# A decoder layer on one core: instructions on separate regions of one tile are declared independent

## The chip, the core and the metric

The kernel runs on one core of one Trainium2 chip. The metric is the time on the device in microseconds (us) of one execution. Five engines work side by side, each through its own list of instructions in order: TensorE (PE in the profile; PEld is its loading of weights), VectorE (DVE), ScalarE (ACT), GpSimd (POOL) and SyncE (SP), which here only issues transfers (DMA). They hold each other back by waits on semaphores, which stand in the program at the instruction that waits.

## The reference

One transformer decoder layer with a mixture of experts, on 32 sequences of 128 tokens with 128 features, in float32, 16 heads of 8:

```python
x = _layernorm(x + _attn(x, x, x, sa_*, causal=True), ln1_g, ln1_b)
x = _layernorm(x + _attn(x, encoder_output, encoder_output, ca_*, causal=False), ln2_g, ln2_b)
x = _layernorm(x + _moe(x, router_w, router_b, e_w1, e_b1, e_w2, e_b2), ln3_g, ln3_b)
```

`_attn` projects queries, keys and values, takes `softmax(q k / sqrt(8))` by head, and projects the result with `wo`. `_moe` routes every token to the best 2 of 8 experts; an expert is 128 to 512, gelu, 512 to 128, with biases; the two results are added with a softmax of the two router weights.

## The kernel before

**Stages.** The 32 sequences form 8 groups of 4 (`gi`). A group goes through self attention (`"s"`) and, two turns later, cross attention (`"c"`); the turns are s0 s1 s2 c0 s3 c1 ... s7 c5 c6 c7, and steps of both kinds are interleaved. Up to about 436 us into the span this attention part runs. Then come 71 blocks of 128 routed rows, each with one expert's weights: transpose the rows (line 1778), move them out of PSUM (1781), first product (1793), gelu (1801), second product (1810), bias (1822), scatter of the results (1827). The blocks overlap, and the layer norms of finished groups lie between them.

**Scores.** Each attention step computes the scores twice. Once by query, from which DVE takes the negated maximum of each row (line 995); the maxima are split into two bfloat16 numbers by POOL (1013, 1019), transposed by PE (1027) and copied by ACT (`nmT`, 1034 to 1038). Then by key, with the maxima added by further matmuls, so that ACT can take the exponentials straight from PSUM (1436) and PE can use them as they lie. All these matmuls are issued by the helper `mm`, so they share line 891; their operands tell them apart.

**One tile with several regions.** The tile `wall` (128 x 8 x 1156 numbers) holds the eight experts' weights at the end. Before that its middle holds three regions of 2048 numbers, `km_t[0]` to `km_t[2]`:

```python
km0 = [KM0 + 4 * G * P * i for i in range(3)]
km_t = [wflat[:, o : o + 4 * G * P].rearrange("p (r n) -> p r n", r=4) for o in km0]
```

Regions 0 and 1 take the masked keys of self attention, of even and odd groups: `masks` (line 724) writes them with four DMAs from `k` (in the profile `wall<-k`; the same helper writes the masked queries, `qm<-q`). Region 2 takes the keys of cross attention split into three bfloat16 parts: `parts` computes them, writes them to `k_d` in memory (861) and `spread` (868) reads them back with four DMAs (`wall<-k_d`). The self steps (`emit_step`, operand `wall,q`) read regions 0 and 1, the cross steps (`emit_cross`, operands `qm` and `wall`) read region 2. What a step reads and what the helpers write for another group thus lie apart, in one tile.

**PSUM.** There are four pairs of banks, `sc0` to `sc3`. A step of scores takes a whole pair (`pairs`); everything else takes half a pair, one bank (`singles`), and at most two pairs are broken up so. Two tasks that have nothing to do with each other may hold the two halves of one tile.

**The order.** Every piece of work is a `Task` with an engine, an estimated duration, a priority, the tasks it depends on (`deps`) and the places it uses (`bufs`). `Plan.run` makes the order of all tasks by a list schedule; in it the two halves of a pair, and the regions of `wall`, are separate places. `Plan.emit` then issues the tasks in this order. The waits are not made by the plan but from the tiles that the issued instructions name: in the program before, an instruction on a part of a tile also waits where an instruction queued earlier touched another part of it, as the rows of the next section but one show.

Of the kernel before, what the change touches and what calls it, by code (L numbers as in the profile page):

```python
# [136 lines left out]


class Task:
    __slots__ = ("eng", "dur", "fn", "deps", "bufs", "prio", "lat", "mode", "use", "ni", "n", "next", "end", "start")  # L140

    def __init__(self, eng, dur, fn, deps, bufs, prio, lat, mode, use, ni):
        self.use, self.ni = use, ni
        self.eng, self.dur, self.fn, self.bufs = eng, dur, fn, bufs
        self.prio, self.lat, self.mode = prio, lat, mode
        self.deps = [d for d in deps if d is not None]
        self.next, self.end, self.start = [], None, None


class Plan:  # L150
# [3 lines left out]
    def __init__(self):  # L154
        self.tasks = []

    def add(self, eng, dur, prio, fn, deps=(), bufs=(), lat=0.0, mode=None, use=0.0, ni=0):
        t = Task(eng, dur, fn, deps, list(bufs), prio, lat, mode, use, ni)
        for b in t.bufs:
            b.left += 1  # L160
        self.tasks.append(t)
        return t
# [100 lines left out]
        self.order = order  # L263
        return max(t.end for _, _, t in order)

    def emit(self):
        for _, _, t in self.order:
            t.fn()


@with_exitstack
def kernel(
# [34 lines left out]
    nc = tc.nc  # L307
# [13 lines left out]
    plan = Plan()  # L321
    add = plan.add
# [89 lines left out]
    t_selc = early("DVE", 0.6, 4.2, c_selc, [t_cols])  # L412
# [123 lines left out]
    bqk = sb([P, 8], "bqk")  # L536
    bqc = sb([P, 1], "bqc")

    def pe(dur, prio, fn, deps, bufs, mode="128x128", use=None, ni=0):
        use = max(dur - 0.18, 0) if use is None else use  # L540
        return add("PE", dur, prio, fn, deps, bufs, mode=mode, use=use, ni=ni or int(dur * 18))

    b = Buf(singles)

# [172 lines left out]
    def masks(dst, src, bufs, prio, deps, two):  # L717

        ts = []
        for q, rs in (("SP", (0, 2)), ("ACT", (1, 3))) if two else (("SP", range(4)),):  # L720

            def fn(q=q, rs=rs):
                for r in rs:
                    (nc.sync if q == "SP" else nc.scalar).dma_start(out=dst.at[r::4, r, :], in_=src()[r::4])

            ts.append(add(q, 0.6 * len(rs), prio, fn, deps, bufs, lat=2.0))
        return ts

    def prepare(kind, gi, n_=1):
# [111 lines left out]
    def parts(w, gi, bank, dep, bcol, t_bias, to, prio):  # L841
# [25 lines left out]
                src = d[:, a[0] : a[0] + 2] if a[1] > a[0] else bc(d[:, a[0]], 1, 2)  # L867
                nc.sync.dma_start(out=view(to)[c::4], in_=src)  # L868

        return [add("SP", 4 * 0.6, prio + 0.06, spread, [tw], [to], lat=5.5)]  # L870

    def sq_cols(tl):

# [109 lines left out]
    def step_use(sq, sk):  # L983
        return (0.43 if sq is not None else 0) + (0.55 if sk is not None else 0)
# [461 lines left out]
    def self_step(sq, sk, i):  # L1446
# [5 lines left out]
        for h in range(2):  # L1452
# [7 lines left out]
            if sk is not None:  # L1460
# [6 lines left out]
            t = pe(  # L1467
                step_time(sq, sk), i + 0.5 * h + PR["score"],
                lambda sq=sq, h=h, qp=qp, sk=sk, kp=kp: emit_step(sq, h, qp, sk, kp), deps, bufs, "32x64",
                use=step_use(sq, sk), ni=step_instr(sq, sk),  # L1470
            )
            if sq is not None:
                last_sq.setdefault(sq[1] % 2, []).append(t)
# [8 lines left out]
    def cross_step(tl, i):  # L1482
# [5 lines left out]
        for h in range(2):  # L1488
            qp = Buf(pairs)
            t = pe(  # L1490
                0.38, i + 0.5 * h + PR["cscore"], lambda h=h, qp=qp: emit_cross(False, h, gi, w, qp),
                [*it.t_q, *it.t_km], [qp, it.qm, it.km], "64x128", use=0.21, ni=16,
            )
            last_sq.setdefault(2, []).append(t)
            ms.append(maximum(tl, h, qp, nm, i + 0.5 * h + PR["cmax"], t))
        transposed_maxima(tl, i, nm, ms)
        i += NL
        for h in range(2):
            kp = Buf(pairs)
            t = pe(  # L1500
                0.6, i + 0.5 * h + PR["ckey"], lambda h=h, kp=kp: emit_cross(True, h, gi, w, kp),
                [*it.nmt[tl], t_selc], [kp, it.qm, it.km, it.nmT, it.pr[w]], "64x128", use=0.42, ni=32,
            )
            last_sq.setdefault(2, []).append(t)
            exponentials(tl, h, kp, t, i + 0.5 * h + PR["cexp"])
# [398 lines left out]
        final(gi, s, 2 if gi == NG - 1 else 1)  # L1904

    plan.run()
    plan.emit()


# [39 lines left out]
```

## Time and profile before

| | |
|---|---|
| median of 3 runs | 665.37 us (664.6, 665.37, 671.98) |
| the profiled execution | 662.87 us, its span 661.2 us |
| mean granted TensorE clock in it | 0.905 |
| PE busy | 513.9 us, 78% of the span |
| DVE, ACT, POOL busy | 425.8, 332.6, 318.5 us |
| attention part | about 0 to 436 us |
| blocks of the experts | about 436 to 640 us |
| tail | 640 to 661 us |

The span is measured from the first instruction to the last; 1.67 us of the execution lie around it. In answers by window the columns are the busy time of each engine with its count of instructions, then the mean granted clock of TensorE (1.00 is full speed), the mean busy share of the DMA engines and the gigabytes per second they moved. In answers on waits a row reads: engine and line, whom it waited for, the total in us, how often, the longest. In a timeline the brackets at the end give the idle time just before and what ended it.

### The profile page before, as it was taken

How to read it: one execution, taken by the hardware profiler on the slowest of the kernel's cores; microseconds unless marked ns; L12 is line 12 of the kernel's file. 1: busy time of each engine (PE TensorE's matmuls, PEld its weight loads, DVE VectorE, ACT ScalarE, POOL GpSimd, SP SyncE). 2: the span in 40 equal slices, each digit the busy share in tenths (PEclk: the TensorE clock that was granted, in tenths of full speed). 3: DMA queues.
4: the chain of work that ended last, by engine and by line, in shares of the span. 5: the costliest groups of instructions: out<-in, count | busy, mean ns of one | idle time of the engine just before them, and what ended most of it. 6: DMA issues, size and time to landing. Idle time of an engine off the chain costs nothing.

```text
span 661.2 us, 20553 instructions
## 1 busy us (share of the span) xinstructions
PE 513.9 (78%) x8055; PEld 397.7 (60%) x8055; DVE 425.8 (64%) x1091; ACT 332.6 (50%) x742; POOL 318.5 (48%) x473
## 2 busy tenths in 40 slices
PE   8997898768777867877798885848579898978830
PEld 5655666546555645654667654637568887877730
DVE  7534769467477668457548876755446557866885
ACT  3352656446256443436545462526146666666642
POOL 8210431422236455225315536746757455767583
PEclk9997999879799977879988987779879999999985
DMA  4552141413213412341532416141222122333331
GB/s 111 155 167 82 55 125 43 129 41 105 83 34 110 118 45 58 106 117 26 134 106 62 129 50 178 48 126 53 77 61 58 57 63 81 105 102 95 107 92 57
DMA packets 55209, 58.67 MB, mean 89 GB/s; under 512 B 7951, under 2 KB 47927, under 8 KB 53064
## 3 DMA queue, kind: packets, MB, share of 16 engines
q1 hardware_dynamic: 50308, 48.49, 25.9%
q0 software_dynamic: 4320, 8.47, 3.8%
q8 instruction: 63, 1.03, 0.7%
q10 hardware_dynamic: 484, 0.39, 0.2%
q14 instruction: 34, 0.28, 0.1%
HBM read 35.69 MB, written 17.90 MB: 81 GB/s over the span
## 4 chain that ended last, share of the span: by engine, by line
PE 44%; DVE 17%; ACT 14%; issue 8%; DMA 7%; POOL 3%; SPq 2%; another core or an unknown queue 2%; DVEq 1%; ACTq 0%; POOLq 0%
PE sc L891 22%; PE sc L1810 5%; ACT pr L1436 5%; PE sc L1793 5%; ACT k L1801 4%; DVE nm L995 4%; DMA wall<-k_d 3%; PE sc L709 2%; PE sc L702 2%; PE sc L788 2%; PE sc L712 2%; SPq L868 2%; DVE y L1867 1%; DVE y L1864 1%
## 5 line engine op out<-in xcount | busy, mean ns | idle before, releaser
L995 DVE TENSOR_REDUCE nm<-sc 128x8 f32<-128x1024 f32 (+1 forms) x112 | 133.3, 1215 | 77.0 <-PE sc L891 71.7
L1436 ACT ACTIVATE pr<-sc 128x1024 f32<-128x1024 f32 x112 | 112.0, 1023 | 103.0 <-PE sc L891 85.3
L1827 POOL DMA_INDIRECT res_d<-o,id x71 | 84.7, 1192 | 53.2 <-DVE o L1822 29.3
L1801 ACT ACTIVATE k<-sc,qm 128x128 f32<-128x128 f32 x284 | 78.5, 379 | 57.0 <-PE sc L1793 35.8
L1810 PE MATMUL sc<-qm,k 128*128 128x128 f32 x568 | 80.0, 285 | 16.7 <-ACT k L1801 9.7
L1810 PEld LDWEIGHTS sc<-qm,k 128*128 128x128 f32 x568 | 70.8, 195 | 25.9 <-ACT k L1801 17.0
L1345 POOL DMA_INDIRECT rows_d<-x,rid x64 | 65.9, 1029 | 35.6 <-issue 21.4
L1793 PE MATMUL sc<-q,qm 128*128 128x128 f32 x568 | 74.5, 284 | 3.6 <-DVE qm L1772 2.3
L1793 PEld LDWEIGHTS sc<-q,qm 128*128 128x128 f32 x568 | 70.4, 200 | 4.5 <-DVE qm L1772 2.6
L891 PE MATMUL sc<-pr,v 128*32 128x128 f32 (+1 forms) x2048 | 66.4, 274 | 6.2 <-issue 2.0
L891 PE MATMUL sc<-wall,q 32*64 32x512 f32 (+1 forms) x512 | 56.1, 530 | 15.8 <-DMA wall<-k_d 15.7
L891 PEld LDWEIGHTS sc<-pr,v 128*32 128x32 f32 x2048 | 52.3, 115 | 17.2 <-issue 7.3
L891 PE MATMUL sc<-qm,k 32*64 32x256 f32 (+1 forms) x512 | 54.1, 515 | 8.1 <-DVE nm L995 4.0
L1772 DVE COPY qm<-wall 128x1156 f32 x71 | 55.3, 779 | 3.5 <-DVE y L1231 1.0
L1822 DVE TENSOR_TENSOR o<-sc,qm 128x128 f32<-128x128 f32 x71 | 20.4, 288 | 50.7 <-PE sc L1810 23.7
L891 PE MATMUL sc<-wall,qm 64*128 64x128 bf16 x512 | 26.8, 238 | 21.4 <-DMA wall<-k 7.0
L1781 ACT ACTIVATE q<-sc,col_b,col_g 128x128 f32<-128x128 f32 x71 | 33.1, 475 | 19.1 <-PE sc L1778 13.5
L1019 POOL CAST nmx<-nm 128x16 bf16<-128x16 f32 x32 | 6.4, 201 | 69.5 <-DVE nm L995 67.8
L1166 ACT ACTIVATE y<-y,rs 128x128 f32<-128x128 f32 x64 | 27.6, 490 | 24.4 <-DVE rs L1158 24.3
L891 PEld LDWEIGHTS <-qm 64*128 64x128 bf16 x512 | 18.6, 103 | 33.9 <-issue 31.8
L1098 DVE STREAM_TRANSPOSE u<-sc 128x512 f32<-128x512 f32 x32 | 22.8, 711 | 21.3 <-PE sc L891 8.9
L891 PE MATMUL sc<-qm,wall 64*128 64x128 bf16 x512 | 28.0, 232 | 6.8 <-ACT pr L1436 3.7
(260 smaller groups left out, 987.2 us busy)
## 6 DMA issues: line engine op xcount, KB each, us to landing
wall<-k_d SPq DMA_DIRECT2D x32, 256.0 KB
qm<-q_d SPq DMA_DIRECT2D x32, 256.0 KB
wall<-in_L_xattn_e_w_dram SPq DMA_DIRECT2D x16, 256.0 KB
pr<-res_d SPq DMA_DIRECT2D x7, 512.0 KB
k_d<-sp SPq DMA_DIRECT2D x8, 384.0 KB
q_d<-sp SPq DMA_DIRECT2D x8, 384.0 KB
xin<-rows_d SPq DMA_DIRECT2D x36, 65.0 KB
xT<-rows_d SPq DMA_DIRECT2D x35, 65.0 KB
```

What stands on the lines that cost most here:

```text
L891: nc.tensor.matmul(out_, lhsT=lhsT, rhs=rhs, start=start, stop=stop, skip_group_check=True)
L995: lambda: nc.vector.tensor_reduce(dst(), src(), AX.X, ALU.max, negate=True), [dep], [pair, nm],
L1098: t = add("DVE", dve(512), prio, lambda: nc.vector.transpose(u1.at, bank.at), [dep], [bank, u1])
L1166: lambda i=i: nc.scalar.activation(to()[:, i, :], y.at[:, i, :], AF.Identity, bias=rs.at[:, 1, i : i + 1], scale=rs.at[:, 0, i : i + 1],),
L1345: ins = nc.gpsimd.indirect_dma_start(out=rows_d[:, :], out_offset=bass.IndirectOffsetOnAxis(ap=rid.at[:, i, k : k + 1], axis=0), in_=x2g[g ...
L1436: lambda: nc.scalar.activation(prb.at[:, 8 * h : 8 * h + 8, :].rearrange("p h q -> p (h q)"), pair.at.rearrange("p b n -> p (b n)"), AF.Ex ...
L1772: nc.vector.tensor_copy(w.at.rearrange("p r n -> p (r n)")[:, 0:WB], flat[:, bass.ds(r, WB)])
L1781: lambda: nc.scalar.activation(xT.at[:, 0:P], bt.at[:, 0:P], AF.Identity, bias=cols["b2"], scale=cols["g2"]),
L1793: nc.tensor.matmul(pp.at[:, 0, c * P : (c + 1) * P], lhsT=wv()[:, c * P : (c + 1) * P], rhs=xT.at[:, 0:P], start=True, stop=True)
L1801: nc.scalar.activation(h.at[:, c, :], pp.at[:, 0, c * P : (c + 1) * P], AF.Gelu, bias=wv()[:, 2 * FF + c : 2 * FF + c + 1],)
L1810: nc.tensor.matmul(pp.at[:, 1, 0:P], lhsT=h.at[:, c, :], rhs=wv()[:, FF + c * P : FF + (c + 1) * P], start=c == 0, stop=c == NFC - 1,)
L1827: ins = nc.gpsimd.indirect_dma_start(out=res_d[:, :], out_offset=bass.IndirectOffsetOnAxis(ap=idb.at[:, 0:1], axis=0), in_=o.at, in_offset ...
```

## The change

A task may carry `apart=(join, off)`: it joins the named group, and it is declared independent of the instructions that joined group `off` before. Four names are used: `masked` (the DMAs of `masks`) against `csteps` (cross steps), and `spread` (the DMAs of `spread`) against `steps` (self steps), in both directions. For the halves of PSUM pairs `emit` makes the groups itself: a task that holds half `j` of a pair is declared independent of what another engine did on half `1 - j`. In both cases dependencies are kept on tasks that stand in `deps` or share a place. The plan, the priorities and the computation stay as they are.

```diff
     def emit(self, nc, tc):
+        of = {}
         for _, _, t in self.order:
+            t.made = made = []
+            nc.push_inst_callback(made.append)
             t.fn()
+            nc.pop_inst_callback()
+            join, off = [t.apart[0]], [t.apart[1]]
+            for b in t.bufs:
+                if isinstance(b.slots, Banks.Kind) and b.slots.single:
+                    entry, j, _ = b.slots.b.of[id(b.at)]
+                    join.append((id(entry[0]), j, t.eng))
+                    off += [(id(entry[0]), 1 - j, e) for e in ("PE", "ACT", "DVE") if e != t.eng]
+            join = {g for g in join if g}
+            off = {g for g in off if g and g in of} - {(*g[:2], e) for g in join if len(g) == 3 for e in ("PE", "ACT", "DVE")}
+            places = {id(b.at) for b in t.bufs}
+            for g in off:
+                keep = [
+                    i for u in of[g] if u in t.deps or any(id(b.at) in places for b in u.bufs) for i in u.made
+                ]
+                for i in made:
+                    tc.declare_no_dep(i, group=str(g), keep=keep, reason="apart within a tile")
+            for g in join:
+                of.setdefault(g, []).append(t)
+                for i in made:
+                    tc.add_to_no_dep_group(str(g), i)
...
-            ts.append(add(q, 0.6 * len(rs), prio, fn, deps, bufs, lat=2.0))
+            ts.append(add(q, 0.6 * len(rs), prio, fn, deps, bufs, lat=2.0, apart=("masked", "csteps")))
...
-        return [add("SP", 4 * 0.6, prio + 0.06, spread, [tw], [to], lat=5.5)]
+        return [add("SP", 4 * 0.6, prio + 0.06, spread, [tw], [to], lat=5.5, apart=("spread", "steps"))]
...
-                use=step_use(sq, sk), ni=step_instr(sq, sk),
+                use=step_use(sq, sk), ni=step_instr(sq, sk), apart=("steps", "spread"),
...
-                [*it.t_q, *it.t_km], [qp, it.qm, it.km], "64x128", use=0.21, ni=16,
+                [*it.t_q, *it.t_km], [qp, it.qm, it.km], "64x128", use=0.21, ni=16, apart=("csteps", "masked"),
```

The order of the instructions is the same on every engine; what differs is the waits. On TensorE, at the self step that reads region 0 (`q2`, the third group) while region 2 is being filled for the first cross group, the program before has this (names in brackets are semaphores: `DMAHW` of transfers, `Activation` of ACT, `DVE` of DVE):

```order
L891 MATMUL sc2_67<-pr2_153,v0_140 32x2x32 x4
L891 MATMUL sc3_68<-qm1_133,k1_138 64x512 [waits DVE_49]
L891 MATMUL sc3_68<-qm1_133,k1_138 64x512 x3
L891 MATMUL sc1_66<-wall_91,q2_131 64x4x64 [waits DMAHW6_49,DMAHW1_49,DMAHW7_49,DMAHW0_49,Activation_49]
L891 MATMUL sc1_66<-wall_91,q2_131 64x4x64 x7
```

and the changed one this:

```order
L918 MATMUL sc2_67<-pr2_153,v0_140 32x2x32 x4
L918 MATMUL sc3_68<-qm1_133,k1_138 64x512 [waits DVE_49]
L918 MATMUL sc3_68<-qm1_133,k1_138 64x512 x3
L918 MATMUL sc1_66<-wall_91,q2_131 64x4x64 [waits Activation_49]
L918 MATMUL sc1_66<-wall_91,q2_131 64x4x64 x7
```

The four waits on transfers are gone there; those four transfers are waited for by the first cross step instead, which stands 998 instructions later in TensorE's list. On TensorE in the blocks of the experts (line 1778 transposes a block's rows into half a pair, line 1810 is the second product) the program before has:

```order
L1778 MATMUL sc1_66<-ident_71,xT0_124 128x128 [waits DMAHW6_49,DVE_49]
L1810 MATMUL sc3_68<-qm0_132,k2_139 128x128 [waits Activation_49]
L1810 MATMUL sc3_68<-qm0_132,k2_139 128x128 x3
L1778 MATMUL sc1_66<-ident_71,xin1_123 128x128 [waits DMAHW7_49,Activation_49]
L1810 MATMUL sc0_65<-qm1_133,k0_137 128x128 x4
```

and the changed one:

```order
L1805 MATMUL sc1_66<-ident_71,xT0_124 128x128 [waits DMAHW6_49,DVE_49]
L1837 MATMUL sc3_68<-qm0_132,k2_139 128x128 [waits Activation_49]
L1837 MATMUL sc3_68<-qm0_132,k2_139 128x128 x3
L1805 MATMUL sc1_66<-ident_71,xin1_123 128x128 [waits DMAHW7_49]
L1837 MATMUL sc0_65<-qm1_133,k0_137 128x128 [waits Activation_49]
L1837 MATMUL sc0_65<-qm1_133,k0_137 128x128 x3
```

The second transpose, into the other half of `sc1`, no longer waits for ACT to have emptied the first half; the wait on ACT that the product behind it needs (for the gelu) now stands at that product.

More of the change, by code (lines that the diff above doesn't have):

```diff
@@ L139 @@
 class Task:
-    __slots__ = ("eng", "dur", "fn", "deps", "bufs", "prio", "lat", "mode", "use", "ni", "n", "next", "end", "start")
+    __slots__ = ("eng", "dur", "fn", "deps", "bufs", "prio", "lat", "mode", "use", "ni", "n", "next", "end", "start", "apart", "made")
     def __init__(self, eng, dur, fn, deps, bufs, prio, lat, mode, use, ni):
@@ L147, in __init__ @@
         self.next, self.end, self.start = [], None, None
+        self.apart, self.made = (None, None), []
 class Plan:
@@ L155, in __init__, with add @@
         self.tasks = []
-    def add(self, eng, dur, prio, fn, deps=(), bufs=(), lat=0.0, mode=None, use=0.0, ni=0):
+    def add(self, eng, dur, prio, fn, deps=(), bufs=(), lat=0.0, mode=None, use=0.0, ni=0, apart=(None, None)):
         t = Task(eng, dur, fn, deps, list(bufs), prio, lat, mode, use, ni)
+        t.apart = apart
         for b in t.bufs:
@@ L264, in run, with emit @@
         return max(t.end for _, _, t in order)
-    def emit(self):
+    def emit(self, nc, tc):
+        of = {}
         for _, _, t in self.order:
+            t.made = made = []
+            nc.push_inst_callback(made.append)
             t.fn()
+            nc.pop_inst_callback()
[18 more added lines that the diff above has]
+                    tc.add_to_no_dep_group(str(g), i)
 @with_exitstack
@@ L537, with pe @@
     bqc = sb([P, 1], "bqc")
-    def pe(dur, prio, fn, deps, bufs, mode="128x128", use=None, ni=0):
+    def pe(dur, prio, fn, deps, bufs, mode="128x128", use=None, ni=0, apart=(None, None)):
         use = max(dur - 0.18, 0) if use is None else use
-        return add("PE", dur, prio, fn, deps, bufs, mode=mode, use=use, ni=ni or int(dur * 18))
+        return add("PE", dur, prio, fn, deps, bufs, mode=mode, use=use, ni=ni or int(dur * 18), apart=apart)
     b = Buf(singles)
@@ L1501, in cross_step @@
                 0.6, i + 0.5 * h + PR["ckey"], lambda h=h, kp=kp: emit_cross(True, h, gi, w, kp),
-                [*it.nmt[tl], t_selc], [kp, it.qm, it.km, it.nmT, it.pr[w]], "64x128", use=0.42, ni=32,
+                [*it.nmt[tl], t_selc], [kp, it.qm, it.km, it.nmT, it.pr[w]], "64x128", use=0.42, ni=32, apart=("csteps", "masked"),
             )
@@ L1906 @@
     plan.run()
-    plan.emit()
+    plan.emit(nc, tc)
 _L = "L0_xattn_"
```

## The prediction

> **What bounds the kernel now.** I read the page first, then who TensorE waited for, then the chain of waits, then windows round the long waits.
>
> ```profile
> PE 513.9 (78%) x8055; PEld 397.7 (60%) x8055; DVE 425.8 (64%) x1091; ACT 332.6 (50%) x742; POOL 318.5 (48%) x473
> ...
> PE 44%; DVE 17%; ACT 14%; issue 8%; DMA 7%; POOL 3%; SPq 2%; another core or an unknown queue 2%; DVEq 1%; ACTq 0%; POOLq 0%
> ```
>
> TensorE is the engine with the most work, and the one that holds most of the chain that ended last. The chain also spends 7% of the span on transfers. What TensorE waited for (engine, line, releaser: us in total, times, longest):
>
> ```profile
> PE sc L891 <- DMA wall<-k_d: 15.7, 5, 4.6
> PE sc L891 <- ACT pr L1436: 14.2, 30, 1.0
> ...
> PE sc L891 <- DVE nm L995: 9.2, 14, 1.7
> PE sc L891 <- DMA wall<-k: 7.0, 3, 3.6
> ...
> PE sc L1778 <- ACT q L1781: 4.8, 13, 2.1
> ...
> PE sc L891 <- DVE u L1098: 2.3, 2, 1.3
> ...
> PE sc L702 <- ACT nmT L1034: 1.8, 3, 1.0
> ...
> PE sc L712 <- ACT k L770: 0.8, 1, 0.8
> ```
>
> The transfers into `wall` stand for 15.7 + 7.0 = 22.7 us in eight waits. The steps that wait in the first row read region 0 or 1, and what lands is region 2; in the fourth row it is the other way round. So these are waits on data that the step does not read. They are on the chain of waits (start, us, what):
>
> ```profile
> 51.58 4.33 DMA wall<-k_d
> ...
> 120.71 4.34 DMA wall<-k_d
> ...
> 135.74 1.91 DMA wall<-k
> ...
> 165.58 5.19 DMA wall<-k_d
> ...
> 246.02 1.91 DMA wall<-k
> ...
> 284.49 3.71 DMA wall<-k_d
> ```
>
> The windows below pair each of the six long waits with the 8 us behind it:
>
> ```profile
> 51.60:56.20 4.60, 0.01 (x1) 0.02 (x1) 0.59 (x2) 0.00 (x0) 0.00 (x0) 0.83 0.76 228
> 56.20:64.00 7.80, 7.79 (x171) 6.06 (x171) 3.75 (x7) 1.99 (x3) 0.78 (x4) 0.66 0.02 4
> 122.10:125.30 3.20, 0.03 (x6) 0.04 (x2) 0.06 (x1) 0.00 (x0) 0.75 (x2) 1.00 0.51 169
> 125.30:133.00 7.70, 7.70 (x121) 5.09 (x123) 3.89 (x8) 3.45 (x5) 3.14 (x7) 0.78 0.01 3
> 134.10:137.80 3.70, 0.10 (x4) 0.04 (x3) 2.69 (x3) 0.37 (x1) 0.83 (x3) 0.84 0.20 74
> 137.80:146.00 8.20, 7.13 (x64) 3.92 (x65) 3.75 (x5) 3.66 (x6) 0.41 (x2) 0.66 0.19 49
> 166.40:170.90 4.50, 0.11 (x8) 0.07 (x5) 0.14 (x1) 0.00 (x0) 0.20 (x1) 0.98 0.69 214
> 170.90:179.00 8.10, 8.02 (x163) 6.10 (x163) 3.48 (x8) 1.29 (x2) 2.38 (x3) 0.59 0.01 2
> 244.80:248.00 3.20, 0.09 (x1) 0.00 (x0) 0.00 (x0) 0.59 (x1) 0.03 (x1) 0.66 0.22 82
> 248.00:256.00 8.00, 7.25 (x81) 4.59 (x83) 5.93 (x9) 3.77 (x7) 3.51 (x7) 0.50 0.03 8
> 285.50:288.30 2.80, 0.03 (x4) 0.00 (x0) 2.25 (x9) 0.12 (x1) 1.14 (x2) 1.00 0.65 211
> 288.30:296.00 7.70, 6.99 (x102) 5.12 (x110) 3.20 (x6) 2.71 (x6) 2.25 (x3) 0.62 0.16 45
> ```
>
> Two things are to be seen. In four of the six waits DVE and ACT stand nearly as still as PE (0.59, 0.06, 0.14, 0.00 us of DVE work): the whole machine waits for one transfer. And behind every wait the granted clock is 0.50 to 0.78, while PE is busy nearly throughout, so each wait is paid for a second time.
>
> **The change part by part.** The order on every engine is the same; waits go, and a few come in their place at later instructions. With durations as they are, no instruction could start later; what can cost something is a duration that changes, or an added wait.
>
> *Waits on regions of `wall`.* All eight lose their reason, 22.7 us. What is late next decides how much is kept. The transfers still have true readers, the cross steps. Weight loads from `qm` begin the cross steps that read the parts of the second, third and fifth group:
>
> ```profile
> 132.70 0.50 PEld L891 LDWEIGHTS <-qm 64*128 64x128 bf16 x17 [0.33 <-issue]
> ...
> 180.77 0.23 PEld L891 LDWEIGHTS <-qm 64*128 64x128 bf16 x8
> ...
> 297.36 0.23 PEld L891 LDWEIGHTS <-qm 64*128 64x128 bf16 x8
> ```
>
> By the chain the parts land at 120.71 + 4.34 = 125.05, 170.77 and 288.20, so they are there 7.7, 10.0 and 9.2 us ahead. PE would come earlier by the wait and by the clock lost behind it (next term): 3.2 + 1.7 = 4.9, 4.5 + 3.3 = 7.8, 2.8 + 2.7 = 5.5. Each is less than the lead, so no new wait on transfers is due. DVE is next: in the windows at 134.1 and 285.5 it worked 2.69 and 2.25 us while PE stood, a backlog that PE would meet. I count these two windows (3.7 + 2.8) by half: 22.7 - 3.25, say 19 us. Bounds: 11, by half of everything, and 22.7.
>
> SP's `spread` drops a wait on self steps as well, and its transfers start a little earlier; I count nothing for that, since their readers do not wait.
>
> *The clock behind the waits.* Busy time times the missing clock in the six windows: 7.79 x 0.34 + 7.70 x 0.22 + 7.13 x 0.34 + 8.02 x 0.41 + 7.25 x 0.50 + 6.99 x 0.38 = 2.65 + 1.69 + 2.42 + 3.29 + 3.63 + 2.66 = 16.3 us. Not all is kept: with a faster PE, DVE (5.93 of 8 us in the window at 248) and ACT are met sooner. I take six tenths, 10 us; bounds 5 and 16.3. The Trainium skill, page "TensorE: Matmul & The Clock Gate", section "HAM oscillation — how this bites in real kernels", would have only idle gaps over about 3.4 us throttle. The rows differ: gaps of 3.2, 3.2 and 2.8 us are followed by 0.78, 0.50 and 0.62. By that rule only the gaps of 4.6, 3.7 and 4.5 us would cost clock, 8.4 us, of which six tenths are 5, and the sum would end at 635; the measurement decides.
>
> *Halves of PSUM pairs, attention part.* Short waits of PE on an engine that empties the other half are among the last three rows on waits: at most 0.8 + 1.8 + 2.3 = 4.9 us. More copies by ACT and DVE start earlier too, but most are not waited for at once. I take 3; bounds 0 and 4.9.
>
> *Halves, expert blocks.* Two blocks' transposes go into the two halves of one pair, and the second waits until ACT has emptied the first:
>
> ```profile
> 504.47 0.33 PE L1778 MATMUL sc<-ident,xin 128*128 128x128 f32 x1 [0.22 <-ACT q L1781]
> ...
> 484.00:555.00 71.00, 64.34 (x499) 58.29 (x497) 42.15 (x101) 42.94 (x145) 41.90 (x34) 0.97 0.23 66
> ```
>
> The row on waits has 13 of these, 4.8 us, of which one is 2.1 us; the others are some 0.22 us each. PE is busy 64.34 of 71 us here, so its short gaps are on the path. The wait that remains behind it, of line 1810 on the gelu, is a true one. I take 3.5; bounds 2 and 4.8.
>
> *Added waits.* The changed program has seven more instructions that only wait (20 more on ACT, 14 fewer on PE, the rest on DVE and SP). The nearest row:
>
> ```profile
> L891 PEldq EVENT_SEMAPHORE  x53: 51/51/4174, 16.3 to 409.0; - x53
> ```
>
> At the median of 51 ns that is 7 x 0.051 = 0.4 us, or 20 x 0.051 = 1.0 us if ACT's were all on the path. I take 0.4.
>
> *Sum.* 19 + 10 + 3 + 3.5 - 0.4 = 35.1 us. The profiled execution took 662.87 us, 661.2 of span and 1.67 around it; it goes to 627.8. It lay 2.5 us under the median of 665.37, so the median goes to 630.
>
> **The rivals.**
>
> *A. The waits go, the clock does not.* If PE's many gaps of under 2 us let the clock fall as often as before, the clock term is lost: 19 + 3 + 3.5 - 0.4 = 25 us, 640. For it:
>
> ```profile
> 300.00:360.00 60.00, 50.48 (x1072) 36.56 (x1074) 38.97 (x93) 33.94 (x55) 26.79 (x48) 0.94 0.33 87
> 360.00:420.00 60.00, 46.03 (x743) 35.27 (x734) 46.32 (x161) 28.08 (x53) 28.96 (x52) 0.83 0.38 110
> ```
>
> Neither stretch has one of the eight waits, and the second still has 0.83. Against it: the first has 0.94. The Trainium skill, same page, section "A second HAM failure mode: psum-queue depth-cycling", describes a clock that swings because PE idles shortly between groups as it cycles through PSUM; that would be this rival, and the row at 360 fits it, the row at 300 does not.
>
> *B. A wait takes the place of the one removed.* PE already waits 14.2 us for ACT's exponentials and 9.2 us for DVE's maxima, in order to get a PSUM pair back. If after each removed wait the next pair were not free, 22.7 us would only change their name, and the PSUM halves alone would count: 3 + 3.5 - 0.4 = 6 us, 659. That the declarations do not take away what they name would end there as well. Against it: DVE and ACT were idle in four of the six waits, so they owed PE nothing; and the waits shown above as changed are gone.
>
> *C. Slower: the clock falls over the whole attention part.* PE reaches the cross steps early and spreads what was one long idle gap over many short ones there, and the clock stays low throughout. Its place is the first 436 us:
>
> ```profile
> 0.00:436.00 436.00, 351.13 (x6802) 250.28 (x6806) 280.01 (x676) 210.85 (x349) 177.08 (x342) 0.91 0.33 96
> ```
>
> At the 0.83 of the row at 360, the same work takes 351.13 x 0.91 / 0.83 = 385 us, 34 more; less the 22.7 it is 11 us slower, 676. It decides from a clock of 351.13 x 0.91 / (351.13 + 22.7) = 0.85 downwards. Against it: PE has less idle time in all, and in the expert blocks, with PE busy nine tenths, the clock is 0.97.
>
> **How the numbers follow.** Forecast 60%, A 25%, B 10%, C 5%. The forecast by its bounds: all terms in full, 22.7 + 16.3 + 4.9 + 4.8 = 48.7, give 617; a cautious set, 15 + 5 + 1 + 2 = 23, gives 642. A reaches, with the waits at their half (11 + 3 + 3.5 = 17.5), to 648. The range 616 to 650 holds the forecast and A and leaves out B and C. Within 1% (6.7 us) is what a measurement of this kernel, with three runs 1.1% apart, can hardly tell from no change. Faster by more: forecast and A, 0.85; B lies within, 0.10; slower, C, 0.05.
>
> **What would show it.** The rows of PE on `wall<-k_d` and `wall<-k` gone or under 2 us in all. The clock of the first 400 us at 0.93 or more, instead of 0.91, and PE's busy time 8 to 16 us lower. The row of line 1778 on line 1781 gone, and two blocks 0.2 us nearer. ACT and DVE busy as before. Wrong would be: new waits on `wall` or `qm` at cross steps (the leads were too short), the rows of PE on ACT 1436 and DVE 995 grown by over 10 us (B), or PE's busy time as before at the same clock (A).

## The result

| | median of the runs | range |
|---|---|---|
| before | 668.21 us | 664.6 to 671.98 |
| changed | 601.33 us | 600.24 to 601.86 |
| ratio | 0.8996 | interval 0.8932 to 0.9061 |

The kernel became faster by 67 us, a tenth. The forecast was 35 us (630, range 616 to 650): the sign was right, the size was not. Four later runs of the changed kernel fell into a slower state (606.69, 608.71, 654.53 and 736.89 us, the last at a clock of 0.58) and are left out of the times below. The profiled execution took 601.86 us, its span 600.1 us: 61 us less than the span of before.

The page of the changed kernel, its line on the engines' busy time, and from the answer on waits the rows of TensorE that are longest now (engine, line, releaser: us in total, times, longest):

```profile
PE 487.0 (81%) x8055; PEld 385.6 (64%) x8055; DVE 422.1 (70%) x1091; ACT 332.3 (55%) x742; POOL 319.1 (53%) x473
```

```profile
PE sc L1837 <- ACT k L1828: 19.1, 24, 5.4
PE sc L918 <- ACT pr L1463: 11.7, 24, 1.0
...
PE sc L918 <- DVE nm L1022: 6.4, 16, 0.9
...
PE sc L918 <- DMA xin<-rows_d: 4.5, 1, 4.5
```

Lines have moved by 27 (891 is 918 now, 995 is 1022; in some kernels below by up to 36). The rows on `wall<-k_d` and `wall<-k`, 22.7 us before, are gone altogether, and no cross step waits for them in their place. The wait of 4.5 us in the last row is that of a step of the last cross group, which reads `qm` and `wall`; the transfer that the row names is not one that it reads, its own `qm` land about then, and the kernel before has the same wait with 3.7 us. PE's busy time fell from 513.9 to 487.0 us, 26.9 us less for the same 8055 matmuls. Weighted by the granted clock it is 461 us before and 459 after, so nearly all of the difference is a faster clock. Its idle time fell from 661.2 - 513.9 = 147.3 to 600.1 - 487.0 = 113.1 us, 34.2 less. 26.9 + 34.2 are the 61.1 us of the span. ACT and DVE worked as long as before (332.3 and 422.1 us against 332.6 and 425.8).

The windows of the attention part and of the blocks of the experts, in the changed kernel (busy time of PE, PEld, DVE, ACT and POOL, then the granted clock, the share of the DMA engines, GB/s):

```profile
0.00:378.00 378.00, 327.47 (x6807) 238.44 (x6808) 276.53 (x674) 209.91 (x347) 177.49 (x342) 0.96 0.39 109
423.00:494.00 71.00, 63.11 (x502) 59.10 (x502) 42.03 (x105) 45.08 (x151) 40.92 (x34) 0.95 0.24 67
```

The first answers to the row 0:436 of before. The same work took 378 us instead of 436, at a clock of 0.96 instead of 0.91. So nearly all of the gain lies in the attention part. The page's line on the clock shows it by slices of a fortieth of the span, before and then after:

```profile
PEclk9997999879799977879988987779879999999985
```

```profile
PEclk9999999999999999997999967697699999999975
```

After the change the clock is full up to 276 us. What is left of the low clock is one stretch there, three around the passage to the experts' blocks (348 to 430 us), and the tail.

Where the time went can be read off by matching the two traces: each TensorE instruction's start before, less the start of the same instruction after, is what had been gained by then.

| place in the trace before, us | gained so far, us | what lies between this row and the one above |
|---|---|---|
| 47.8 | 2.4 | |
| 61.2 | 10.3 | wait of 4.6 us at 51.6 |
| 119.8 | 11.7 | |
| 142.9 | 22.3 | waits of 3.2 at 122.1 and 3.7 at 134.1 |
| 163.6 | 22.6 | |
| 176 | 29.6 | wait of 4.5 at 166.4 |
| 232.7 | 34.4 | none of the eight waits that is longer than 2 us |
| 244 | 40.0 | none; short waits for ACT, and the clock (below) |
| 250.7 | 44.1 | wait of 3.2 at 244.8 |
| 282 | 45.1 | |
| 293.5 | 49.6 | wait of 2.8 at 285.5 |
| 440 | 57.6 | none |
| 555 | 61.2 | blocks of the experts |

The steps with the six long waits sum to 7.9 + 10.6 + 7.0 + 4.1 + 4.5 = 34 us. In the passage to the blocks, from 425 to 490 us, the figure swings between 56 and 62; from there to 555 it climbs evenly by 3.5, which is what the blocks give. The remaining 61 - 34 - 4 = 23 us lie in the attention part away from the long waits, where the forecast had 3.

### The profile page after: what moved, and what is told of

Same layout as the page of the kernel before. It is cut to its first block, busy times and chain, and to the rows that moved or that the text cites. A ratio compares the mean times of both kernels' runs of the same rounds, so it can differ in the third digit from the quotient of the medians.

```text
span 600.1 us, 20560 instructions
## 1 busy us (share of the span) xinstructions
PE 487.0 (81%) x8055; PEld 385.6 (64%) x8055; DVE 422.1 (70%) x1091; ACT 332.3 (55%) x742; POOL 319.1 (53%) x473
## 5 line engine op out<-in xcount | busy, mean ns | idle before, releaser
L1854 POOL DMA_INDIRECT res_d<-o,id x71 | 83.7, 1179 | 50.7 <-DVE o L1849 22.5
L1837 PE MATMUL sc<-qm,k 128*128 128x128 f32 x568 | 80.2, 287 | 23.6 <-ACT k L1828 19.1
L918 PEld LDWEIGHTS sc<-pr,v 128*32 128x32 f32 x2048 | 50.8, 111 | 21.2 <-issue 11.6
L1799 DVE COPY qm<-wall 128x1156 f32 x71 | 57.4, 809 | 3.5 <-DVE y L1258 1.0
L918 PE MATMUL sc<-qm,k 32*64 32x256 f32 (+1 forms) x512 | 52.6, 502 | 5.6 <-ACT pr L1463 3.2
L918 PE MATMUL sc<-wall,q 32*64 32x512 f32 (+1 forms) x512 | 53.3, 500 | 0.6 <-issue 0.3
L1808 ACT ACTIVATE q<-sc,col_b,col_g 128x128 f32<-128x128 f32 x71 | 33.2, 479 | 10.1 <-PE sc L1805 5.0
L1125 DVE STREAM_TRANSPOSE u<-sc 128x512 f32<-128x512 f32 x32 | 22.6, 707 | 17.4 <-PE sc L918 12.6
L918 PE MATMUL sc<-wall,qm 64*128 64x128 bf16 x512 | 25.3, 228 | 11.6 <-DMA xin<-rows_d 4.5
```

What stands on the lines that cost most here:

```text
L918: nc.tensor.matmul(out_, lhsT=lhsT, rhs=rhs, start=start, stop=stop, skip_group_check=True)
L1799: nc.vector.tensor_copy(w.at.rearrange("p r n -> p (r n)")[:, 0:WB], flat[:, bass.ds(r, WB)])
L1808: lambda: nc.scalar.activation(xT.at[:, 0:P], bt.at[:, 0:P], AF.Identity, bias=cols["b2"], scale=cols["g2"]),
L1837: nc.tensor.matmul(pp.at[:, 1, 0:P], lhsT=h.at[:, c, :], rhs=wv()[:, FF + c * P : FF + (c + 1) * P], start=c == 0, stop=c == NFC - 1,)
L1854: ins = nc.gpsimd.indirect_dma_start(out=res_d[:, :], out_offset=bass.IndirectOffsetOnAxis(ap=idb.at[:, 0:1], axis=0), in_=o.at, in_offset ...
```

## The experiments

The runs were made in several comparisons, which fall into two groups: in one the kernel before takes 667 to 668 us, in the other 633. Some expectations below speak of different chips, but the record has the same chip number, 6, beside a comparison of each group. Ratios to the kernel before agree between the groups (changed kernel: 0.8996, 0.9079 and 0.8967 in the first, 0.9059 in the second); absolute times are compared only within a group.

### Regions of `wall` alone, halves of PSUM alone

The first kernel makes no groups for the halves, the second passes no `apart` to the tasks on `wall`:

```diff
-                if isinstance(b.slots, Banks.Kind) and b.slots.single:
+                if False and isinstance(b.slots, Banks.Kind) and b.slots.single:
```

> Only the declarations on regions of the weights' tile; the halves of PSUM pairs keep their waits. Theory 1 (the eight waits on transfers cost their length and the whole of the slow clock behind them, 22.7 + 16.3 us, and the clock lost elsewhere follows from them): 40 to 50 us of the 67 are had, 618 to 628. Theory 2 (the forecast's terms were right for these waits, 29 us, and the excess comes from the PSUM halves, which act all along): 635 to 642.

Measured: 592.20 us against 632.54, ratio 0.9368 (0.9328 to 0.9409).

```diff
-            ts.append(add(q, 0.6 * len(rs), prio, fn, deps, bufs, lat=2.0, apart=("masked", "csteps")))
+            ts.append(add(q, 0.6 * len(rs), prio, fn, deps, bufs, lat=2.0))
...
-        return [add("SP", 4 * 0.6, prio + 0.06, spread, [tw], [to], lat=5.5, apart=("spread", "steps"))]
+        return [add("SP", 4 * 0.6, prio + 0.06, spread, [tw], [to], lat=5.5)]
...
```

(and the same at the three tasks of steps)

> Only the declarations on halves of PSUM pairs; the waits on the transfers into the weights' tile stay. Theory 1: 6 to 15 us gained, 653 to 662. Theory 2: 25 to 35 us gained, 633 to 643.

Measured: 612.96 us, ratio 0.9664 (0.9622 to 0.9705).

So `wall` alone brings 40 us of 633, the halves alone 20, and the two add: 0.9368 x 0.9664 = 0.905, where the whole change has 0.906 in this group. The forecast had 29 and 6.5. Both terms were too small, the second by a factor of three. On the 668 us of the result these ratios are 42 and 22 us: `wall` alone came out as theory 1 had it, the halves alone lie between the two theories.

### The waits and the clock behind them apart

To pay the wait and not the clock, overwritten matmuls of 128x512 are put ahead of the steps that hold the six long waits, 93 in all, into the PSUM pair that the step overwrites afterwards. First in the kernel before:

```diff
+            if t.tag in FILL:
+                armed = ("step" if t.tag[0] == "parts" else "cstep", FILL[t.tag])
+            elif armed and t.tag and t.tag[0] == armed[0]:
+                for _ in range(armed[1]):
+                    nc.tensor.matmul(t.tag[1].at[:, 0, :], lhsT=ones, rhs=bc(ones, 1, 4), start=True, stop=True)
+                armed = None
             t.fn()
```

> The kernel before with all its waits, and 93 more matmuls of 128x512 whose results are overwritten: 11 to 20 of them, some 0.21 us each, just ahead of the steps that sit out the six long waits, so that TensorE is busy for most of each wait and waits as long as before in all. This prices the clock by itself. Theory 1: the slow stretches behind the six waits go, 16 us or more, about 648 to 652. Rival (the slow clock is covered by the other engines): 5 us or less, 663 or more; were the added work itself on the path, slower, up to 688.

Measured: 621.68 us against 632.54, ratio 0.9835 (0.9803 to 0.9867): 10.9 us for the clock alone, between what theory 1 and its rival said.

Then the same on the kernel with only the halves declared, beside that kernel without them and the changed kernel, in one comparison:

> Only the PSUM halves declared, the eight waits on regions of wall stay; the reference for the next run on the same chip. Both theories: 0.96 to 0.972 of the kernel before, as on the other chip (0.966).

> As the run before it, with 93 matmuls of 128x512 whose results are overwritten, put ahead of the steps that hold the six long waits on wall, so that TensorE has work during the wait and the clock has no reason to fall; the waits stay. What lies between this and the run before is the clock's price, what lies between this and the changed kernel the waits' own. Theory 1 (the waits were kept nearly in full and the clock at what the forecast took, some 10 us): 10 to 14 us below the run before, 26 to 32 us above the changed kernel. Rival (the waits are worth the forecast 19 us, the clock more than the six windows show): 20 us or more below the run before, 20 us or less above the changed kernel.

> The changed kernel on the same chip as the two runs before it, as their other end. Both theories: 0.895 to 0.91 of the kernel before.

| | us | step |
|---|---|---|
| before | 667.06 | |
| halves only | 641.84 (640.24 to 649.36), ratio 0.9642 | -25.2 |
| halves only, waits filled | 630.47 (626.81 to 632.28), ratio 0.9417 | -11.4: the clock |
| changed | 599.27 (two runs, 597.61 and 600.92), ratio 0.8967 (0.8891 to 0.9044) | -31.2: the waits |

Theory 1 holds in both steps. By the ratios they are 15.0 and 30.0 us, with intervals of some 5. Matching the profiled executions as above gives 8 to 11 us for the clock and, against the changed kernel of the result, 30 for the waits, all of it by 280 us, where the last long wait is past. The page and the waits of the kernel with only the halves:

```profile
PE 501.2 (79%) x8055; PEld 393.8 (62%) x8055; DVE 425.3 (67%) x1091; ACT 331.7 (52%) x742; POOL 318.8 (50%) x473
```

```profile
PE sc L918 <- DMA wall<-k_d: 17.5, 5, 4.5
...
PE sc L918 <- DMA wall<-k: 7.7, 3, 3.6
```

With the waits filled, the page and the group of the 93 matmuls (busy us and mean ns behind the bar; they are pipelined, so that 93 times the mean is more than the busy time):

```profile
PE 508.8 (81%) x8148; PEld 394.8 (63%) x8148; DVE 426.5 (68%) x1091; ACT 330.8 (52%) x742; POOL 317.8 (50%) x473
```

```profile
L281 PE MATMUL sc<-ones 128*128 128x512 bf16 x93 | 21.1, 379 | 0.4 <-DVE nm L1031 0.2
```

Without the 21.1 us of filling, PE is busy 487.7 us: 13.5 less than the 501.2 of the run beside it, and nearly what the changed kernel has (486.5 to 487.0). So filling the gaps gave back the clock that the waits on `wall` cost, and by the times and the traces 8 to 11 of the 13.5 us reached the end. What was left, some 30 us, are the waits: 25.2 us as the rows count them, and with the gaps filled 21.1 of filling and 6.0 that are still in the rows, 27.1. They were kept in full; the 3 us beyond them stay open. The waits are longer here than the 22.7 us of the kernel before, since PE comes to them earlier by more than the transfers do.

The Trainium skill, page "TensorE: Matmul & The Clock Gate", section "HAM oscillation — how this bites in real kernels", would have only gaps over about 3.4 us throttle the clock. By that rule the three shorter waits cost nothing, and the prediction worked out 5 us for it. The runs, with 8 to 15 us, lie nearer to the rows, which gave 10, and the clocks of 0.78, 0.50 and 0.62 behind those three waits contradict the rule directly.

One wait alone, that for the parts of the third cross group, put back into the changed kernel:

```diff
+            if t.tag == ("parts", 2):
+                join = []
             join = {g for g in join if g}
```

> The changed kernel with one wait put back: the self steps again wait for the parts of the keys of the third cross group (the wait that took 4.5 us in the profile before). Theory 1: that wait and the clock behind it, 7 to 8 us, 608 to 609. Rival (only the wait itself counts): 4 to 5 us, 605 to 606. If such a wait is mostly made up for later: under 2 us, 603.

Measured: 573.96 us (572.89 to 577.39), ratio 0.9077 (0.9035 to 0.9119); the changed kernel in the same group has 572.17 and 0.9059. Its profile has the wait:

```profile
PE sc L921 <- DMA wall<-k_d: 4.9, 2, 4.7
```

The intervals overlap: 1.8 us is measured where a wait of 4.7 us stands. Matching this trace with that of the changed kernel shows what became of the rest. At the wait 7.4 us are lost, from 1.1 us behind at 140 us to 8.5 at 170, which is the wait and the clock, as theory 1 had it. Of these 8.5 us, 5.2 are left at 350 us and 2.9 at the end, so most of it was made up for later, as the third expectation had it. What made it up was not tried.

### Where the 20 us of the halves lie

The kernels of this part keep the regions of `wall` declared and limit for whose instructions the halves are declared:

```diff
-                    off += [(id(entry[0]), 1 - j, e) for e in ("PE", "ACT", "DVE") if e != t.eng]
+                    off += [(id(entry[0]), 1 - j, e) for e in ("PE", "ACT", "DVE") if e != t.eng and t.eng == "PE"]
```

The condition at the end reads `t.eng == "PE"` (TensorE's instructions alone), `t.eng != "PE"` (ACT's and DVE's), `t.prio >= 60` (the tasks of the blocks), `t.eng != "ACT"`, `t.eng != "DVE"`, `t.eng == "ACT"` or `t.eng == "DVE"`.

> The changed kernel itself, beside the variants of this comparison, since chips differ in their times. Theory 1 (the gain is what the waits, the clock and the halves are worth, whatever the chip): a ratio to the kernel before of 0.89 to 0.91. Rival (the 10% was a peculiarity of the chip on which the kernel before took 668 us): 0.92 or more.

> The regions of wall stay declared; of the PSUM halves only TensorE's instructions are declared independent, those of ACT and DVE wait for the other half as before. With no halves at all the ratio was 0.937, with all of them 0.90, so the halves are worth some 3.7%, 24 us, where 6.5 were forecast. Theory 1 (what was forecast too small is the copies of ACT and DVE that start earlier, which the forecast left out as not waited for at once): a ratio of 0.92 to 0.93, a third of the 3.7% or less. Rival (it is PE's own waits and the clock behind them): 0.91 or less.

> The opposite: of the PSUM halves only the instructions of ACT and DVE are declared independent, TensorE's wait for the other half as before. Theory 1: 0.91 or less, two thirds of the halves' 3.7%. Rival (PE's own waits): 0.925 or more.

> The regions of wall stay declared; the PSUM halves are declared only for the tasks of the experts' blocks and of the layer norms among them. Theory 1 (the expert part was sized rightly at 3.5 us, the attention part holds the rest): a ratio of 0.928 to 0.934. Rival (the blocks hold most of it): 0.915 or less.

| halves declared for | us (before: 666.98) | ratio |
|---|---|---|
| the blocks only | 623.54 | 0.9359 (0.9294 to 0.9424) |
| TensorE | 617.33 | 0.9285 (0.9215 to 0.9354) |
| ACT and DVE | 610.77 | 0.9157 (0.9095 to 0.9220) |
| all | 601.07 | 0.9079 (0.9006 to 0.9152) |

With the halves in the blocks only, the time is that of `wall` alone (0.9368) within the intervals, which are too wide to show a term of 3.5 us; so the attention part holds some 20 us (623.54 - 601.07 = 22.5 by the times, 18.7 by the ratios). The ratio is a little above what theory 1 had (0.934) and far from its rival. TensorE's instructions alone came out as theory 1 expected (0.9285). Those of ACT and DVE alone, 0.9157, miss its 0.91 and the rival's 0.925 alike; they bring 12.8 us, about twice the 6.2 of TensorE's. The matched traces show the blocks apart from this: where TensorE waits for the other half again (third row), the lead over the first row falls from 16.2 us at the passage to 12.6 at the end of the blocks, while the changed kernel keeps its 21. Those 3.6 us are the blocks' term, forecast at 3.5.

What ACT was held up by can be read in the rows on groups of the page before, by who ended its idle time. Ahead of the bars the group, its copies and their count; then busy us and mean ns; then the idle us ahead of it and what ended it:

```profile
L1034 ACT COPY nmT<-sc 128x128 bf16<-128x128 bf16 x32 | 8.3, 267 | 14.3 <-PE sc L1027 5.9 <-PE sc L709 4.4 <-DVE u L851 1.9
...
L847 ACT ACTIVATE sp<-sc,bqk 128x512 bf16<-128x512 f32 x8 | 5.5, 686 | 13.0 <-PE sc L709 7.1 <-PE sc L712 4.9 <-PE sc L788 0.7
...
L1038 ACT COPY nmT<-sc 128x128 bf16<-128x128 bf16 x16 | 4.3, 266 | 7.0 <-PE sc L891 4.1 <-DVE u L1098 1.7 <-PE sc L1027 0.7
```

and after, in the same order:

```profile
L1061 ACT COPY nmT<-sc 128x128 bf16<-128x128 bf16 x32 | 8.3, 267 | 9.8 <-PE sc L1054 9.3
...
L874 ACT ACTIVATE sp<-sc,bqk 128x512 bf16<-128x512 f32 x8 | 5.5, 688 | 2.3 <-PE sc L736 2.0 <-ACT y L1193 0.2
...
L1065 ACT COPY nmT<-sc 128x128 bf16<-128x128 bf16 x16 | 4.3, 266 | 2.5 <-PE sc L1054 2.3
```

The copies `nmT` read what the transposes of line 1027 (1054 now) write, and nothing else. Before, their idle time was also ended by the products of the exponentials with the values (891), the projections (709) and DVE's transposes (`u`): these belong to the other half. After, one releaser is left in the rows, the true one. Worked out from the start times in the trace before (an instruction's start, less the later of its engine's last end and its true producers' ends), ACT's work on a half stood late behind the other half 33 times, 26.6 us in all, and DVE's 28 times, 19.6 us, against 5.8 us for TensorE itself.

The longest case, in the timeline of before (start, us, engine, line, what):

```profile
236.45 2.07 PE L709 MATMUL sc<-xT,wkc 128*128 128x512 f32 x2 [1.16 <-ACT xT L757]
...
241.29 1.58 PE L712 MATMUL sc<-xT,wqsp 128*128 128x256 f32 x4
...
244.23 0.66 PE L702 MATMUL sc<-ident,y 128*128 128x128 f32 x4 [1.03 <-ACT k L770]
```

```profile
242.91 0.69 ACT L847 ACTIVATE sp<-sc,bqk 128x512 bf16<-128x512 f32 x1 [4.86 <-PE sc L712]
243.50 0.68 ACT L770 ACTIVATE k<-sc,bqk 128x512 f32<-128x512 f32 x1
```

and after:

```profile
200.35 1.13 PE L736 MATMUL sc<-xT,wkc 128*128 128x512 f32 x2
...
202.92 1.03 PE L739 MATMUL sc<-xT,wqsp 128*128 128x256 f32 x4
```

```profile
202.53 0.67 ACT L874 ACTIVATE sp<-sc,bqk 128x512 bf16<-128x512 f32 x1
203.12 0.69 ACT L797 ACTIVATE k<-sc,bqk 128x512 f32<-128x512 f32 x1
```

ACT needs the product with `wkc`, ready at 236.45 + 2.07 = 238.52. It began at 242.91, when the product with `wqsp` in the other half had ended, 4.4 us late, and behind it the copies `k` and `q` were late too, until PE stood for `k`. After, ACT starts while `wqsp` is still to come. The gain so far rose from 34.4 to 40.0 us here, but only 1.0 us of it is TensorE's wait for this copy `k`: two more short waits of TensorE for ACT just before it, 0.5 and 1.2 us, are gone too, and the other 2.9 us are clock, which before was 0.50 from 235.6 to 242.4 us.

Which of the two engines carries it was asked from both sides, with one engine's waits put back and with one engine alone freed:

> The changed kernel, but ACT's instructions wait for the other half of a PSUM pair as before (TensorE's and DVE's do not, the regions of wall stay declared). In the profile of the kernel before, ACT's work on a half stood late behind the other half 33 times in the attention part, 26.6 us in all, DVE's 28 times, 19.6 us. Theory 1 (each engine's lateness counts in proportion, 14 us of time for 46 us of lateness): 6 to 11 us above the changed kernel. Rival (only ACT's copies feed TensorE's next step, so they carry everything): 13 us or more above it.

> The same for DVE: its instructions wait for the other half as before, ACT's and TensorE's do not. Theory 1: 4 to 8 us above the changed kernel. Rival (ACT carries everything): within 2 us of it.

> The changed kernel on the same chip as the three runs before it, as their reference. Both theories: 0.895 to 0.91 of the kernel before.

> The regions of wall stay declared; of the PSUM halves only ACT's instructions are declared independent. Without halves the ratio was 0.937, with ACT's and DVE's 0.916, with all 0.90. With ACT's or DVE's waits alone put back, the changed kernel lost 1.3 and 4.2 us, much less than their share of the lateness. Theory 1 (the two stand in for each other: their late copies lie one behind the other in the same turns, and freeing either brings most of it): 0.925 or less. Rival (the lateness of ACT alone does not count at all): 0.932 or more.

> The same with DVE's instructions alone declared independent. Theory 1: 0.925 or less. Rival (only both together bring it): 0.932 or more.

All of them, with `wall` alone, are of one group (before 632.5 to 633 us). The last column is what the matched trace had gained on `wall` alone by the end of its attention part (at 405.6 us):

| halves declared for | us | ratio | gained at 405.6 us |
|---|---|---|---|
| none (`wall` alone) | 592.20 | 0.9368 (0.9328 to 0.9409) | 0 |
| ACT | 586.04 | 0.9214 (0.9166 to 0.9262) | 4.9 |
| DVE | 582.08 | 0.9164 (0.9113 to 0.9214) | 7.4 |
| TensorE and ACT | 576.67 | 0.9116 (0.9074 to 0.9157) | 11.9 |
| TensorE and DVE | 573.74 | 0.9056 (0.9001 to 0.9111) | 13.3 |
| all | 572.17 | 0.9059 (0.9013 to 0.9105) | 17.1 |

By the medians ACT's waits put back cost 1.6 us, DVE's 4.5; freed alone they bring 6.2 and 10.1. Put back, ACT's waits thus cost far less than the 6 us or more that theory 1 had and the 13 of its rival, so neither held; DVE's lie in theory 1's 4 to 8. The ratios of the last two runs met what theory 1 expected of them (0.925 or less), that the two engines stand in for each other. The last column does not bear that out: there the parts add, some 5 us for ACT, 7 for DVE and 6 to 7 for TensorE (13.3 - 7.4 and 11.9 - 4.9), 18 to 19 in all against 17.1. In proportion to lateness, as theory 1 of the first two runs had it, ACT should have had more than DVE; it has less. What differs between the columns arises behind the attention part, and there the executions of one kernel differ by several us (568.4 to 577.35 for the fifth row). So in the attention part of these traces, one execution each, every engine carries about a third; whether ACT's share reaches the end when DVE's is there, these runs leave open.

Where TensorE gained by it can be read from its waits for copies. Three of the larger rows in the kernel with the halves in the blocks only:

```profile
PE sc L918 <- DVE u L1125: 2.3, 2, 1.3
...
PE sc L729 <- ACT nmT L1061: 1.8, 3, 1.0
...
PE sc L736 <- ACT xT L784: 1.2, 1, 1.2
```

Of these three the kernel with all halves has left:

```profile
PE sc L729 <- ACT nmT L1061: 0.5, 1, 0.5
```

Up to the first block, TensorE's waits for such copies by ACT and DVE sum to 15.4 us without and 5.8 with the halves of the attention part; its waits for exponentials and maxima fell from 27.0 to 24.4, all its idle time from 60.0 to 49.5. The clock is in it too: PE was busy 493.5 us with the halves in the blocks only and 486.5 with all of them, so 7 of the 22.6 us between these two spans (620.6 and 598.0) are clock. In the 633 group, from `wall` alone to the changed kernel, the waits for copies fell alike (16.6 to 5.7 us) and those for exponentials and maxima more (26.5 to 20.2), but no clock came with it there: up to the first block PE was busy 314.9 and 316.2 us.

### Filling the gaps that are left

In the changed kernel TensorE stands at the passage to the blocks, and the clock is at 0.50 for 20 and 10 us behind it. Two gaps there were filled in the same way, at the PE tasks number 419 and 451:

```diff
+            if t.eng == "PE":
+                at += 1
+                if at in FILL:
...
+                    for _ in range(FILL[at]):
+                        nc.tensor.matmul(p[:, 0:512], lhsT=ones, rhs=bc(ones, 1, 4), start=True, stop=True)
```

> The changed kernel with 29 overwritten matmuls ahead of two instructions at the passage to the experts' blocks, where TensorE still stands for 4.5 and 2.3 us and the clock is 0.50 for 20 and 10 us behind it. Theory 1 (the clock behind an idle gap is paid for wherever TensorE has work waiting): 2 to 7 us faster than the changed kernel. Rival (there TensorE waits for the other engines anyhow, and a full clock only makes it wait longer): within 1.5 us.

This run held 61 such matmuls, not 29; the 32 others stood where they wait for the gelu themselves. It took 607.68 us against 599.27, ratio 0.9082 (0.9022 to 0.9141) against 0.8967, and says nothing on the question. Its repetition with 29:

> The changed kernel with 29 overwritten matmuls ahead of two instructions at the passage to the experts' blocks. The run e12 of this name held 61: 32 more stood ahead of two second products, where they wait for the gelu themselves and cover no gap. Theory 1 (the clock behind an idle gap is paid for wherever TensorE has work waiting): 2 to 7 us faster than the changed kernel. Rival (there TensorE waits for the other engines anyhow): within 1.5 us.

Measured: 574.62 us against 572.17, ratio 0.9085 (0.9045 to 0.9125) against 0.9059 (0.9013 to 0.9105): no gain, so theory 1 is not borne out. The rival's 1.5 us are missed as well, on the slower side. The windows of this kernel, and below them the first of the changed kernel, show what became of it:

```profile
335.00:353.00 18.00, 12.82 (x134) 7.98 (x136) 12.28 (x42) 4.88 (x12) 11.93 (x20) 0.86 0.50 137
351.00:362.00 11.00, 9.80 (x175) 7.84 (x171) 6.87 (x30) 6.56 (x10) 8.70 (x17) 0.53 0.11 33
```

```profile
335.00:353.00 18.00, 12.09 (x155) 9.81 (x157) 14.31 (x48) 7.13 (x14) 13.33 (x24) 0.61 0.43 120
```

The first 18 us have a clock of 0.86 instead of 0.61, but PE did not get further in them (134 matmuls, 20 of them filling, against 155), and the next 11 us have 0.53. Here PE waits for others, and a better clock finds little to run. The test is not a clean one: matched with the changed kernel, this run loses 2.3 us where the first filling stands, so the filling took longer than the gap, and regains 0.9 us of it by 348 us. Whether a filling that fits the gap would gain stays open.

## Why the prediction was right and wrong

- **What bounds the kernel.** Right: TensorE, held by transfers into regions that its steps do not read. The rows on them are gone, and the leads were long enough: no cross step waits for `wall` in the changed kernel (in two of the variants below it, up to 1.0 us in all).
- **Waits on regions of `wall`, 19 us.** Too small: 30 to 31 us measured, above the upper bound of 22.7. Two steps failed. The windows at 134.1 and 285.5, with 2.69 and 2.25 us of DVE work in them, were counted by half because DVE would be late next; the traces show no such new wait (PE's waits for DVE's maxima fell from 9.2 to 6.4 us). And the 22.7 was no upper bound: a wait for something with a time of its own grows when the work ahead of it gets faster, to 25.2 us with the halves declared and 27.1 with the clock restored too. The last 3 us stay open.
- **The clock behind the waits, 10 us.** Right, 8 to 15 us by the measures above, though the six tenths were a guess. What the prediction gave as a sign of it was not: PE's busy time fell by 26.9 us, not 8 to 16. By the pages, 501.2 - 487.7 = 13.5 of it belongs to the waits on `wall`, 513.9 - 501.2 = 12.7 to the halves in this group, for which the prediction had counted no clock.
- **Halves of PSUM pairs, attention part, 3 us (0 to 4.9).** This is the step that failed most: some 20 us. The bound "at most 0.8 + 1.8 + 2.3 = 4.9 us" took three of TensorE's rows on waits for copies; in the trace of before all such waits up to the first block sum to 16.6 us, and 6.6 are left in the changed kernel. The sentence "More copies by ACT and DVE start earlier too, but most are not waited for at once" put aside 46 us of late copies, and it is copies that TensorE waited for, in many short waits at many lines. With the halves declared, the waits for copies fell by 10 us, those for exponentials and maxima by 3, and 7 us of clock came back in one group; in the other it was 11 and 6, and no clock. The page showed it in the rows on groups, as releasers that the copy does not read.
- **Halves, expert blocks, 3.5 us.** Right: 3.6 by the matched traces; the runs are too coarse to show it. The row of line 1778 on line 1781 is gone in the changed kernel; with `wall` alone it is still there:

```profile
PE sc L1805 <- ACT q L1808: 4.7, 19, 0.6
```

- **Added waits, 0.4 us.** Too small to be seen in any run.
- **The sum.** Where 35 us were forecast, the halves brought 25.2, the clock behind the waits 11.4 and the waits 31.2 by the medians of one comparison, 67.8 us in all. The spans of the profiled executions (661.2, 638.5, 630.5 and 600.1 us) give 22.7, 8.0 and 30.4, 61.1 in all. By either, the shortfall is in two terms, the waits on `wall` and the halves.
- **Rival A** (the clock stays): the clock of the attention part rose to 0.96. The Trainium skill, page "TensorE: Matmul & The Clock Gate", section "A second HAM failure mode: psum-queue depth-cycling", on which it leaned, tells of a clock that swings because TensorE idles shortly between groups of matmuls. The traces here have low stretches behind short pauses too (last section), but they became fewer when the waits went, not more. **Rival B** (another wait in their place): PE's waits on ACT 1436 and DVE 995 fell, from 14.2 to 11.7 and 9.2 to 6.4. Only the wait on the gelu in the blocks grew, from 9.7 to 19.1 us, 5.4 of it in the pause of ACT that the last section tells of; in the 633 group it is 9.9 with `wall` alone and 11.4 changed. **Rival C** (slower): never near.
- **The range** reached down to 616 because its lower end took all terms at their bounds as they stood in the trace of before; two of these bounds, 22.7 and 4.9, were not bounds.

## What to carry to other kernels

A wait on the busiest engine is the visible part; false dependencies also delay the copies on the other engines, and the page shows these as idle time ended by an instruction whose output the waiting one does not read. Sum that idle time on every engine before putting an edit down as small, and check for each releaser whether it is the producer. On the busiest engine, add up all waits for such copies, whatever their lines, before calling a sum of a few rows a bound. The waits for transfers cost their length and the clock behind them here, and grew when the work ahead of them was made faster; one of them alone was mostly made up for.

## What the hardware showed besides

**In these traces the clock follows the share of busy time rather than the length of a gap.** In the traces of before and after all stretches at 0.50, but the last, which the end cuts off, last multiples of 3.41 us (3.4, 6.8, 10.2, 13.7, 17.1, 20.5). Counting TensorE's busy time in the 3.41 us ahead of each stretch within the attention part: from 0 up to 2.5 us, with a longest gap of only 0.4 to 0.7 us in six cases. One of them in the changed kernel, in windows of that length and then the stretch:

```profile
269.90:273.30 3.40, 3.40 (x125) 3.00 (x120) 3.18 (x11) 1.02 (x1) 1.54 (x3) 1.00 0.51 161
273.30:276.70 3.40, 2.09 (x30) 0.94 (x24) 1.47 (x7) 1.26 (x2) 2.55 (x3) 1.00 0.19 61
276.70:283.50 6.80, 5.68 (x66) 5.00 (x68) 2.85 (x9) 2.51 (x4) 0.36 (x1) 0.50 0.59 169
```

PE was busy 2.09 of 3.4 us, in short pieces, and the next 6.8 us ran at half the clock. In six traces (before, after, `wall` alone, halves alone and two more of the changed kernel) every window that lost the clock held at most 2.8 us of work, and every one with under 1.5 us lost it; between lies a band in which both happen. Back to full it went only after windows with about 3.0 us of work or more, and not after all of these. So a fifth of a window idle could be enough to lose the clock, and a nearly full one was needed to get it back. This would explain how many short waits, as those behind the halves, cost clock at all. It was read from traces, not tried by a run.

**The same kernel takes 667 us in one group of runs and 633 in the other,** the changed one 601 and 572. By the matched traces of the changed kernel, 13 of the 28 us arise in one place behind 406 us, where ACT stands without a wait that the profile shows; 4 of them are regained by 437 us. The instruction that begins at 424.12 us in the 667 group, behind a pause of 11.94 us, begins at 393.31 in the 633 group, behind 1.16 (timeline of ACT, first the one and then the other):

```profile
411.04 1.14 ACT L1828 ACTIVATE k<-sc,qm 128x128 f32<-128x128 f32 x4 [2.34 <-PE sc L1837]
424.12 1.14 ACT L1828 ACTIVATE k<-sc,qm 128x128 f32<-128x128 f32 x4 [11.94 <-issue]
```

```profile
393.31 1.14 ACT L1828 ACTIVATE k<-sc,qm 128x128 f32<-128x128 f32 x4 [1.16 <-issue]
...
397.06 1.14 ACT L1828 ACTIVATE k<-sc,qm 128x128 f32<-128x128 f32 x4 [1.13 <-issue]
```

The kernel before has the same pause in the 667 group (9.11 us at 481.81). What makes it there and not in the other group stays open.
